# One ring of five PSUM places through the whole program

## The chip, the cores and the metric

The kernel runs on one core of a Trainium2 chip. The metric is the time of one execution on the device in microseconds; several executions are made and the median is given. Beside them one execution is recorded by the hardware profiler, with a start and a length for each instruction of each engine, and for each packet of each DMA queue.

The core has a matrix engine (TensorE, "PE" in the profile), a vector engine (VectorE, "DVE"), a scalar engine (ScalarE, "ACT"), GpSimd ("POOL") and a sync engine ("SP") that here only issues DMAs. TensorE writes its products to PSUM, which has eight banks; a tile of 128 x 512 float32 fills one bank. VectorE or ScalarE reads a product out of its bank, and only then may the next product be written there. Each engine works through its own instructions in a fixed order and waits on semaphores for the others.

## The reference

`x` is 4 x 1024 x 2048 in float32. The block is an adaptive-norm layer with two halves:

```python
mod = (silu(c) @ wmod).reshape(4, 6, 1, -1)            # c: 4 x 2048, wmod: 2048 x 12288
sa, ca, ga, sb, cb, gb = mod[:, 0] ... mod[:, 5]       # ga, gb held away from zero
h = layernorm(x) * (1 + ca) + sa
x = x + ga * (causal_conv(h, K) + D * h)               # K: 2048 taps of a state space model
h = layernorm(x) * (1 + cb) + sb
x = x + gb * (h @ W.T + bias + sum_e w_e (h @ A_e.T) @ Bf_e.T)
```

The convolution runs along the 2048 features of each of the 4096 tokens. `K` comes from 64 complex state parameters by a Cauchy sum at 2048 frequencies and an inverse Fourier transform. The feed forward half has one 2048 x 2048 matrix `W` and sixteen low-rank updates of rank 16.

## The kernel before

The work is done in two stages, and TensorE does nearly all of it as float16 pairs: a float32 operand is split into a high part and a low residue, and three products (high-high, high-low, low-high) stand for one.

*Modulation.* `section(sec)` (sections 0 to 5) does sixteen steps; a step loads a 1 MB tile `wm` of `wmod` from SP's queue and multiplies it in four column groups into `modps` (L325), one PSUM bank of its own. Six weight tiles are in stock for sections 1, 0 and 2, which come first; 4, 3 and 5 are spread over the later rows with three tiles. After the last step ScalarE copies `modps` to `mrow`, four transposes `mtp` (L339) turn it into columns, and VectorE makes `ca`. From `ca` the early scale `cae` is made (`early_scale`, by way of a maximum over partitions on GpSimd).

*The taps.* `toeplitz` runs `s4`, whose few products write `s4cs`, `s4sp`, `s4rp` and `s4kp`; the 2048 taps go to DRAM, `kd`, and come back in two halves as a matrix `kb` of shifted rows (GpSimd's queue, L261). Four products with a reversing matrix write `kbps` (L276); VectorE and ScalarE copy it back to `kb` and make the three float16 pairs `kh`, `kl` of the convolution's families.

*Convolution.* 32 rows of 128 tokens, r = 0 to 31. `conv_prep` normalises a row to `n`, transposes it in four groups of four 128 x 128 transposes, each group into a tile `tp` (L579); ScalarE reads the group in four instructions with the modulation's scale and shift into `t` (L583), VectorE adds pairs to `sm`, and both are split into `hc` and `hs`. `conv_mm` does two halves q of 1024 outputs; each half has three families of products (L616): family 0 into `ya`, which ScalarE copies to `qs` (L629); family 2 into `yb`, which VectorE adds to `qs`; then family 1 onto the same `ya`. So a tile `ya` lives through all three families. A family in the first half has 12 products, 1280 columns times three; in the second half it has 24. VectorE applies the gate and adds `x`. `conv_post` stores the row to DRAM, `x1d`, and sums its square on ScalarE (L666) for the second norm.

*Merging.* Between the rows `merges` prepares the low-rank factors and does eight chunks c: eight tiles `lps` of six low-rank products each (L494), which VectorE adds to the loaded weights `we` (L496); ScalarE scales them, and seven sums of quarter blocks go to DRAM as float16 pairs, `wcd`.

*Feed forward.* A unit u is 256 tokens; there are 16, done for two halves q of the columns. `left` transposes a unit's rows (tiles `tp`, L706) and makes the seven left operands; `ffn_unit` does the seven products of 24 matmuls each (L756) into three tiles X, Y and Z, with ScalarE and VectorE combining them. The first unit's `left` runs during rows 30 and 31 of the convolution.

*PSUM before.* In the first stage: two tiles for `ya` and two for `yb` (pool `cps`), three tiles in pool `tps` for everything else (`tp`, `mtp`, `lps`, `kbps` and the small products), one for `modps`. After the last row the pools are closed and two others opened: five tiles `acc` for the products of the feed forward, two `tps` for its transposes.

*What sets the order.* The program is written as generators that yield to each other (`PLAN` and `tick` say which part of the next row, of the merging or of the modulation is taken at which point of a row). A scheduler then orders each engine's instructions by priority and by its own estimate of when operands and tiles are ready, and it hands out the tiles of a pool to whatever it places next. `tc.issue_after` and `tc.high_priority` steer it in places; the taps' steps have high priority. So a change of pools changes the order in which instructions stand on each engine. What a tile's next user waits for is the last reader of the previous user.

Of the kernel before, what the change touches and what calls it, by code (L numbers as in the profile page):

```python
# [24 lines left out]
P = 128  # L25
# [9 lines left out]
class Net:  # L35
    def __init__(self, ctx, tc, io):
        self.ctx, self.tc, self.nc, self.io = ctx, tc, tc.nc, io
        self.cst = ctx.enter_context(tc.tile_pool(name="cst", bufs=1))
        self.dram = ctx.enter_context(tc.tile_pool(name="scr", bufs=1, space=DRAM))
    def psum(self, stack, name, bufs):  # L40
        return stack.enter_context(self.tc.tile_pool(name=name, bufs=bufs, space=PSUM))

    def const(self, name, shape, dt=F32):
        return self.cst.tile(shape, dt, tag=name, name=name)
# [30 lines left out]
    def s4(self, pool):  # L75
# [66 lines left out]

        nl = T([P, 2], "s4nl")
        tsc(nl, lam, -1.0, None, MUL)
        rp = self.tps.tile([P, 8, 16], F32, tag="t", name="s4rp")
        w = 512
        yield
        cps = [[self.cps.tile([P, w], F32, tag=t, name="s4cs") for t in ("pa", "pb")] for _ in range(2)]
        for n in range(2):
            for i, ps in enumerate(cps[n]):  # L150
                nc.tensor.matmul(ps, one, cs[:, i, ds(n * w, w)], start=True, stop=True)
# [83 lines left out]
    def toeplitz(self, pool):  # L235
        nc, v = self.nc, self.nc.vector
        rev = pool.tile([P, P], F32, tag="rev", name="rev")
        nc.gpsimd.memset(rev, 0.0)
        nc.gpsimd.affine_select(
            out=rev, in_=rev, compare_op=ALU.not_equal, fill=1.0, base=1 - P, pattern=[[1, P]], channel_multiplier=1  # L240
        )
        kk = pool.tile([P, 16], F32, tag="kk", name="kk")
        yield from self.s4(pool)
        v.tensor_copy(kk, self.kp)
        dt = pool.tile([1, 1], F32, tag="dt", name="dt")
        nc.scalar.dma_start(out=dt, in_=self.io["D"].unsqueeze(0))
        v.tensor_tensor(kk[0:1, 0:1], kk[0:1, 0:1], dt, ADD)
        m = pool.tile([P, 1], F32, tag="km", name="km")
        v.tensor_reduce(m, kk, AX.X, ALU.max, apply_absolute_value=True)
        s, self.kinv = self.pow2(self.cst, self.allmax(pool, m, 1, "km"), 1, "ks")  # L250
        v.tensor_scalar(kk, kk, s, None, MUL)
        kd = self.dram.tile([P + D], F32, tag="kd", name="kd")
        z = pool.tile([1, P], F32, tag="kz", name="kz")
        v.memset(z, 0.0)
        nc.gpsimd.dma_start(out=kd[0:P].unsqueeze(0), in_=z)
        nc.gpsimd.dma_start(out=kd[P:].rearrange("(a b) -> a b", b=16), in_=kk)

        kb = pool.tile([P, D], F32, tag="kb", name="kb")
        for h in range(2):
            src = bass.AP(tensor=kd.tensor, offset=kd.offset + 1 + 1024 * h, ap=[[1, P], [1, 1024]])  # L260
            nc.gpsimd.dma_start(out=kb[:, ds(1024 * h, 1024)], in_=src)  # L261
        self.kb = kb
        yield


        kv = kb.rearrange("p (m e t) -> p m e t", e=2, t=P)
        ev, od = kv[:, :, 0, :], kv[:, :, 1, :]
        kf, self.kf = {}, {}
        for f in (0, 2, 1):
            kf[f] = [self.kpool.tile([P, HC, P], F16, tag=f"k{x}{f}", name=f"k{x}{f}") for x in "hl"]  # L270
        for half in range(2):
            m = ds(4 * half, 4)
            for q in range(2):
                ps = self.tps.tile([P, 512], F32, tag="t", name="kbps")
                sl = ds(1024 * half + 512 * q, 512)
                nc.tensor.matmul(ps, rev, kb[:, sl], start=True, stop=True)  # L276
                (v.tensor_copy if q else nc.scalar.copy)(kb[:, sl], ps)
            for f in (0, 2, 1):
                hi, lo = (x[:, m] for x in kf[f])
                if f == 0:  # L280
                    src = ev[:, m]
                else:
                    src = pool.tile([P, 2, 512], F32, tag="kdif", name="kdif")
                    src = src[:, 0].rearrange("p (c t) -> p c t", t=P)
                    if f == 2:
                        v.tensor_tensor(src, od[:, m], ev[:, m], SUB)
                    elif half:
                        v.tensor_tensor(src, od[:, 3 : HC - 1], ev[:, m], SUB)
                    else:
                        v.tensor_scalar(src[:, 0:1], ev[:, 0:1], -1.0, None, MUL)  # L290
                        v.tensor_tensor(src[:, 1:], od[:, 0:3], ev[:, 1:4], SUB)
                nc.scalar.copy(hi, src)
                v.tensor_tensor(lo, src, hi, SUB)
            self.kf = {f: [x.rearrange("p m t -> p (m t)") for x in y] for f, y in kf.items()}
            yield
# [179 lines left out]
    def merge(self, pool, tmp, c):  # L475
        nc, v = self.nc, self.nc.vector
        lf = tmp.tile([P, 2, 2, P], F32, tag="laf", name="laf", bufs=2)
        nc.sync.dma_start(out=lf, in_=self.io["A"][c])
        la = tmp.tile([P, 2, 2, 2, P], F16, tag="lac", name="lac")
        for k in range(2):  # L480
            v.tensor_scalar(lf[:, k], lf[:, k], self.lsa[:, k : k + 1], None, MUL)
        nc.scalar.copy(la[:, 0], lf)
        v.tensor_tensor(la[:, 1], lf, la[:, 0], SUB)
        we = tmp.tile([P, 2, D], F32, tag="we", name="we")
        for h in range(2):
            nc.sync.dma_start(out=we[:, h], in_=self.io["WT"][ds(P * (c + HC * h), P), :])
        for h in range(2):
            for q in range(4):
                ps = self.tps.tile([P, 512], F32, tag="t", name="lps")
                osl = ds(512 * q, 512)  # L490
                n = 0
                for k in range(2):
                    for x, y in ((0, self.bh), (0, self.bl), (1, self.bh)):
                        nc.tensor.matmul(ps, la[:, x, k, h], y[:, k, osl], start=(n == 0), stop=(n == 5))  # L494
                        n += 1
                v.scalar_tensor_tensor(we[:, h, osl], ps, self.linv, we[:, h, osl], MUL, ADD)  # L496
                yield

        m = pool.tile([P, 4], F32, tag="wem", name="wem")
        for h in range(2):  # L500
            for q in range(2):
                j = tmp.tile([P, 1024], F32, tag="wct", name="wsq")
                i = 2 * h + q
                nc.scalar.activation(j, we[:, h, ds(1024 * q, 1024)], AF.Square, accum_out=m[:, i : i + 1])
        mm = pool.tile([P, 1], F32, tag="wmm", name="wmm")
        v.tensor_reduce(mm, m, AX.X, ADD)
        nc.scalar.activation(mm, mm, AF.Sqrt)
        s, inv = self.pow2(pool, mm, 1, "wes")
        for h in range(2):
            v.tensor_copy(self.winv[:, c + HC * h : c + HC * h + 1], inv)  # L510
            for q in range(2):
                sl = ds(1024 * q, 1024)
                nc.scalar.activation(we[:, h, sl], we[:, h, sl], AF.Copy, scale=s)
            yield
        b11, b12 = we[:, 0, 0:1024], we[:, 0, 1024:2048]
        b21, b22 = we[:, 1, 0:1024], we[:, 1, 1024:2048]

        def put(i, t):
            hl = tmp.tile([P, 2, 2, 512], F16, tag="wch", name="wch", bufs=2)
            tv = t.rearrange("p (q n) -> p q n", n=512)  # L520
# [12 lines left out]
        v.tensor_tensor(b12, b22, b12, SUB)  # L533
        put(6, b12)
        yield
        v.tensor_tensor(b11, b12, b11, ADD)
        put(5, b11)
        yield
        v.tensor_tensor(b21, b21, b11, SUB)
        put(3, b21)  # L540
        yield
# [55 lines left out]
    def conv_mm(self, pl, hs, x, tick, early, pace, y=None):  # L597
# [25 lines left out]

        for q in range(2):
            jj = slice(4 * q, 4 * q + 4)
            pa = self.cps.tile([P, 4, P], F32, tag="pa", name="ya")
            family(pa, 0, q, True)
            qs = pl["t"].tile([P, 4, P], F32, tag="qs", name="qs")
            self.lasta = nc.scalar.copy(qs, pa)  # L629
            tick()  # L630
            pb = self.cps.tile([P, 4, P], F32, tag="pb", name="yb")
            family(pb, 2, q, True)
            self.lastv = v.tensor_tensor(yv[:, jj, 1, :], pb, qs, ADD)
            if not early:
# [215 lines left out]
def net(ctx: ExitStack, tc: tile.TileContext, io):  # L850
# [8 lines left out]
    def pool(stack, name, bufs, side="left"):  # L859
        return stack.enter_context(tc.tile_pool(name=name, bufs=bufs, side=side, reuse_waits="tile"))  # L860

    left, right, p2, ps1 = ExitStack(), ExitStack(), ExitStack(), ExitStack()
    k.cps = k.psum(ps1, "cps", 2)
    k.tps = k.psum(ps1, "tps", 3)
    k.mps = k.psum(ps1, "mps", 1)
    pl = {}
    wmp = pool(right, "wm", WM, "right")
    msm = pool(right, "msm", 1, "right")
# [271 lines left out]
    gens = [next_left(1)]  # L1140
    take(gens[0], 1)
    left.close()
    ps1.close()
    k.acc = k.psum(p2l, "acc", ACC)
    k.tps = k.psum(p2l, "tps", TPS)

    for name in ("v", "o", "e", "g"):
        pr[name] = pool(p2l, "p2" + name, 5 if name == "o" else 1)
# [88 lines left out]
```

## Time and profile before

| | us |
|---|---|
| median of three executions | 2143.35 (2140.45 to 2143.99) |
| the profiled execution | 2143.08 |
| its span, first to last instruction | 2141.3 |
| convolution stage | 0 to about 920 |
| feed forward stage | about 920 to 2139 |

The engines' busy time is counted once where instructions overlap. Matmuls are pipelined, so the length shown for one (0.38 us for 512 columns) is longer than the distance to the next (0.213 us). A float32 product other than a transpose shows as two records, so a modulation step of four products shows as eight. A line of a timeline reads: start, length, engine, line, operation, what is written and read, shape, count, and in brackets the idle time before it with what ended it. A line of waits reads: who waited, for whom, us in total, times, the longest. A line by stretch gives, for PE, PEld (weight loads), DVE, ACT and POOL, the busy time and the count of instructions, and then the granted clock of TensorE, the mean busy share of the DMA engines, and GB/s.

### The profile page before, as it was taken

What the parts mean: (1) busy time and instruction counts of PE and PEld (TensorE: products, weight loads), DVE (VectorE), ACT (ScalarE), POOL (GpSimd) and SP (SyncE); (2) the same over time, 40 slices, a digit from 0 to 9 for tenths busy, and PEclk for the clock granted to TensorE, in tenths of its full rate; (3) what the DMA queues carried; (4) which work ended last, traced back from release to release, by engine and by line L of the source; (5) the groups of instructions that cost most, each with busy time, mean ns of one, the idle gap of its engine ahead of it and who ended that gap; (6) DMA issues with size and microseconds to landing.
All of it is one profiled execution on the core that took longest, in us unless ns stands there. A gap on an engine that the chain in (4) does not pass through costs nothing.

```text
span 2141.3 us, 28488 instructions
## 1 busy us (share of the span) xinstructions
PE 2075.5 (97%) x11121; PEld 1022.2 (48%) x11121; DVE 1310.7 (61%) x2360; ACT 924.9 (43%) x1703; POOL 7.2 (0%) x19
## 2 busy tenths in 40 slices
PE   6998999999999999999999999999999999999999
PEld 1434544554545555644545545545444444444444
DVE  6529889888998999756565565565432323332323
ACT  1425776765676768755454454555200000000000
POOL 0000000000000000000000000000000000000000
PEclk8999999999999999999999999999999999999999
DMA  9993768677775556387465564564794545555542
GB/s 402 421 382 136 262 236 298 218 280 284 298 255 197 186 203 246 133 335 274 180 242 188 190 240 180 202 239 178 270 353 162 188 154 171 164 164 167 177 154 73
DMA packets 127813, 486.22 MB, mean 227 GB/s; under 512 B 13672, under 2 KB 14088, under 8 KB 96446
## 3 DMA queue, kind: packets, MB, share of 16 engines
q1 hardware_dynamic: 126624, 479.65, 61.6%
q10 hardware_dynamic: 526, 2.63, 0.3%
q8 instruction: 87, 1.43, 0.3%
q0 software_dynamic: 528, 2.11, 0.2%
q14 instruction: 48, 0.39, 0.1%
HBM read 329.04 MB, written 155.30 MB: 226 GB/s over the span
## 4 chain that ended last, share of the span: by engine, by line
PE 61%; issue 27%; DVE 6%; DMA 3%; ACT 2%; SPq 0%; POOL 0%; POOLq 0%; DVEq 0%; ACTq 0%
PE fZ L756 23%; PE fX L756 15%; PE fY L756 15%; PE tp L706 3%; PE ya L616 2%; PE modps L325 2%; DMA wm<-in_wmod 1%; PE yb L616 1%; ACT t L583 1%; DMA x<-x1d 1%; DVE st L548 1%; DVE hc L594 0%; DVE lf L719 0%; DVE y L643 0%; ACT x L666 0%
## 5 line engine op out<-in xcount | busy, mean ns | idle before, releaser
L756 PEld LDWEIGHTS <-lf 128*128 128x128 f16 x5400 | 528.4, 98 | 621.2 <-issue 3.4
L756 PE MATMUL fZ<-w,lf 128*128 128x512 f16 (+1 forms) x2328 | 513.8, 377 | 1.3 <-ACT p L764 0.8
L756 PE MATMUL fX<-w,lf 128*128 128x512 f16 x1536 | 342.8, 379 | 1.4 <-DVE y L642 1.4
L756 PE MATMUL fY<-w,lf 128*128 128x512 f16 x1536 | 342.0, 379 | 0.0
L616 PEld LDWEIGHTS <-hc 128*128 128x128 f16 x2304 | 214.8, 98 | 212.4 <-issue 46.8
L774 DVE TENSOR_TENSOR xo<-xo,gb 128x512 f32<-128x512 f32 x128 | 87.6, 689 | 238.5 <-DMA xo<-x1d 226.4
L583 ACT ACTIVATE t<-tp,sa,ca 128x128 f32<-128x128 f32 x480 | 189.6, 476 | 38.8 <-PE tp L579 38.6
L616 PE MATMUL ya<-kh,hc 128*128 128x512 f16 (+3 forms) x768 | 192.2, 328 | 9.4 <-ACT qs L629 9.4
L616 PE MATMUL yb<-kh,hc 128*128 128x512 f16 (+3 forms) x768 | 193.4, 328 | 1.9 <-DVE hc L594 1.4
L616 PE MATMUL ya<-kh,hs 128*128 128x512 f16 (+3 forms) x768 | 194.6, 328 | 0.7 <-ACT y L640 0.7
L764 ACT COPY p<-fZ 128x512 f32<-128x512 f32 x64 | 37.2, 582 | 285.4 <-PE fZ L756 272.1
L616 PEld LDWEIGHTS <-hs 128*128 128x128 f16 x1152 | 107.2, 98 | 106.8 <-issue 28.3
L764 ACT COPY p<-fX 128x512 f32<-128x512 f32 x32 | 18.8, 586 | 317.9 <-PE fX L756 242.8
L708 ACT ACTIVATE gt<-tp,sb,cb 128x256 f32<-128x256 f32 x256 | 125.0, 576 | 62.4 <-PE tp L706 60.8
L325 PE MATMUL modps<-wm,sct 128*32 128x512 f32 x768 | 118.1, 653 | 17.1 <-DMA wm<-in_wmod 9.9
L616 PE MATMUL ya<-kl,hc 128*128 128x512 f16 (+3 forms) x384 | 125.7, 327 | 0.0
L616 PE MATMUL ya<-kl,hs 128*128 128x512 f16 (+3 forms) x384 | 125.6, 327 | 0.0
L616 PE MATMUL yb<-kl,hc 128*128 128x512 f16 (+3 forms) x384 | 125.6, 327 | 0.0
L779 DVE TENSOR_TENSOR fin<-fX,gb 128x512 f32<-128x512 f32 x32 | 22.1, 691 | 127.5 <-PE fX L756 127.4
L579 PE MATMUL tp<-ident,n 128*128 128x128 f32 x512 | 76.9, 276 | 16.2 <-DVE n L558 6.8
L594 DVE TENSOR_TENSOR hc<-t,hc 128x512 f16<-128x512 f32 x128 | 87.3, 682 | 7.2 <-ACT hc L593 7.0
L494 PE MATMUL lps<-lbh,lac 128*128 128x512 f16 x256 | 86.4, 380 | 4.8 <-DVE we L496 2.6
(274 smaller groups left out, 2219.8 us busy)
## 6 DMA issues: line engine op xcount, KB each, us to landing
wm<-in_wmod SPq DMA_DIRECT2D x96, 1024.0 KB, 8.3
lfd<-lf SPq DMA_DIRECT2D x112, 512.0 KB, 3.3
lf<-lfd SPq DMA_DIRECT2D x112, 512.0 KB, 3.9
x<-in_x SPq DMA_DIRECT2D x32, 1024.0 KB, 8.2
x1d<-y SPq DMA_DIRECT2D x32, 1024.0 KB, 5.2
x<-x1d SPq DMA_DIRECT2D x32, 1024.0 KB, 7.7
xo<-x1d SPq DMA_DIRECT2D x128, 256.0 KB, 3.7
out<-xo SPq DMA_DIRECT2D x127, 256.0 KB, 2.8
```

The source lines that it names most:

```text
L325: self.last = self.nc.tensor.matmul(self.modps[32 * g : 32 * g + 32, :], self.sct[:, j].rearrange("p r b -> p (r b)"), w[:, ds(512 * g, 512)],
L494: nc.tensor.matmul(ps, la[:, x, k, h], y[:, k, osl], start=(n == 0), stop=(n == 5))
L579: nc.tensor.transpose(tp[:, k], n[:, ds(P * (c0 + k), P)], self.ident)
L583: nc.scalar.activation(t[:, k], tp[:, k], AF.Identity, bias=self.sa[:, c, b : b + 1], scale=self.ca[:, c, b : b + 1],)
L594: self.lastlo = v.tensor_tensor(lo[:, sl], src, hi[:, sl], SUB)
L616: self.lastc = nc.tensor.matmul(pf[:, o:512], h, self.kf[f][z][:, ds(k0, 512 - o)], start=first, stop=(i == last and (x, z) == (1, 0)), sk ...
L706: nc.tensor.transpose(tp[:, c, r], xs[r][:, ds(P * (c0 + c), P)], self.ident)
L708: nc.scalar.activation(t[:, c0 + c], tp[:, c], AF.Identity, bias=self.sb[:, c0 + c, b : b + 1], scale=self.cb[:, c0 + c, b : b + 1],)
L756: nc.tensor.matmul(ps[name][:, cols], lf[i][:, k, x, :], wc[i][k // 4][:, k % 4, y, cols], start=(first and n == 0), stop=(n == 3 * HC - 1 ...
L764: nc.scalar.copy(t, ps[name])
L774: v.tensor_tensor(x, x, self.gbias[:, h], ADD)
L779: v.tensor_tensor(t, cv, self.gbt[:, h], MUL)
```

## The change

The pools of PSUM are opened once, for the whole program: a ring `acc` of five tiles, `tps` of two, `mps` of one. The families of the convolution (`ya`, `yb`), the low-rank products (`lps`), the reversing products (`kbps`) and the taps' `s4cs` and `s4rp` take tiles from `acc`, in one name "a" that the feed forward's X, Y and Z go on using. The transposes, and a few small products (`s4sp`, `s4kp`, `mtp`, `gsp`, `gst`, `gps`), stay in `tps`, which has two tiles instead of three in the first stage. The pools are no longer closed and opened between the stages. No instruction is added or removed.

```diff
+        self.acc = ctx.enter_context(tc.tile_pool(name="acc", bufs=ACC, space=PSUM))
+        self.tps = ctx.enter_context(tc.tile_pool(name="tps", bufs=TPS, space=PSUM))
+        self.mps = ctx.enter_context(tc.tile_pool(name="mps", bufs=1, space=PSUM))
...
-        rp = self.tps.tile([P, 8, 16], F32, tag="t", name="s4rp")
+        rp = self.acc.tile([P, 8, 16], F32, tag="a", name="s4rp")
...
-        cps = [[self.cps.tile([P, w], F32, tag=t, name="s4cs") for t in ("pa", "pb")] for _ in range(2)]
+        cps = [[self.acc.tile([P, w], F32, tag="a", name="s4cs") for _ in range(2)] for _ in range(2)]
...
-                ps = self.tps.tile([P, 512], F32, tag="t", name="kbps")
+                ps = self.acc.tile([P, 512], F32, tag="a", name="kbps")
...
-                ps = self.tps.tile([P, 512], F32, tag="t", name="lps")
+                ps = self.acc.tile([P, 512], F32, tag="a", name="lps")
...
-            pa = self.cps.tile([P, 4, P], F32, tag="pa", name="ya")
+            pa = self.acc.tile([P, 4, P], F32, tag="a", name="ya")
...
-            pb = self.cps.tile([P, 4, P], F32, tag="pb", name="yb")
+            pb = self.acc.tile([P, 4, P], F32, tag="a", name="yb")
...
-    k.cps = k.psum(ps1, "cps", 2)
-    k.tps = k.psum(ps1, "tps", 3)
-    k.mps = k.psum(ps1, "mps", 1)
...
-    ps1.close()
-    k.acc = k.psum(p2l, "acc", ACC)
-    k.tps = k.psum(p2l, "tps", TPS)
```

`ACC` is 5 and `TPS` is 2, as before.

More of the change, by code (lines that the diff above doesn't have):

```diff
@@ L39, in __init__ @@
         self.dram = ctx.enter_context(tc.tile_pool(name="scr", bufs=1, space=DRAM))
-    def psum(self, stack, name, bufs):
-        return stack.enter_context(self.tc.tile_pool(name=name, bufs=bufs, space=PSUM))
+        self.acc = ctx.enter_context(tc.tile_pool(name="acc", bufs=ACC, space=PSUM))
+        self.tps = ctx.enter_context(tc.tile_pool(name="tps", bufs=TPS, space=PSUM))
+        self.mps = ctx.enter_context(tc.tile_pool(name="mps", bufs=1, space=PSUM))
     def const(self, name, shape, dt=F32):
@@ L860, in pool @@
         return stack.enter_context(tc.tile_pool(name=name, bufs=bufs, side=side, reuse_waits="tile"))
-    left, right, p2, ps1 = ExitStack(), ExitStack(), ExitStack(), ExitStack()
-    k.cps = k.psum(ps1, "cps", 2)
-    k.tps = k.psum(ps1, "tps", 3)
-    k.mps = k.psum(ps1, "mps", 1)
+    left, right, p2 = ExitStack(), ExitStack(), ExitStack()
     pl = {}
```

## The prediction

> **What bounds the kernel now.** I read the page first, then TensorE's waits, then busy time by stretch, then TensorE's timeline at the start and around row 18.
>
> ```profile
> PE 2075.5 (97%) x11121; PEld 1022.2 (48%) x11121; DVE 1310.7 (61%) x2360; ACT 924.9 (43%) x1703; POOL 7.2 (0%) x19
> ```
>
> TensorE is busy for 97% of the span, and no product goes away: time moves only where TensorE's idle time grows or shrinks. Where that is, by stretch (PE busy, ..., granted clock, DMA share, GB/s):
>
> ```profile
> 0.00:50.00 50.00, 32.31 (x152) 5.97 (x152) 30.69 (x114) 6.98 (x11) 4.09 (x13) 0.86 0.98 400
> 50.00:150.00 100.00, 94.56 (x603) 39.86 (x603) 42.06 (x102) 33.94 (x92) 1.30 (x3) 0.97 0.99 403
> 150.00:300.00 150.00, 135.35 (x806) 72.32 (x803) 126.96 (x285) 97.58 (x208) 1.06 (x2) 0.95 0.59 219
> 300.00:920.00 620.00, 599.02 (x3686) 321.84 (x3685) 550.24 (x1131) 437.22 (x889) 0.78 (x1) 1.00 0.65 239
> 920.00:2141.00 1221.00, 1214.29 (x5884) 582.20 (x5881) 560.76 (x730) 349.22 (x505) 0.00 (x0) 1.00 0.57 201
> ```
>
> From 920 us on (feed forward) only 7 us are idle, and the change leaves that stage's places as they were. The stage before it idles for about 59 us, 18 of them before 50 us. What those waits are (us in total, times, longest):
>
> ```profile
> PE ya L616 <- ACT qs L629: 9.4, 8, 2.3
> ...
> PE tp L579 <- ACT t L583: 5.8, 3, 2.8
> PE tp L579 <- DVE we L496: 3.5, 3, 1.6
> ...
> PE lps L494 <- DVE we L496: 2.6, 2, 1.9
> PE lps L494 <- ACT t L583: 2.2, 4, 0.6
> ```
>
> All but the first line are waits for a PSUM place, since `tp` and `lps` share three tiles; so is the first feed forward product's wait for VectorE's `y` (1.4 us, once).
>
> **The change, part by part.** Four parts.
>
> (1) *Low-rank products leave the transposes' ring.* The place waits above sum to 5.8+3.5+2.6+2.2+1.4 = 15.5 us. I count them all as removed: in the new ring each `lps` takes a place whose last reader lies 7 to 13 us of TensorE work back. The changed order also puts six low-rank products (1.28 us) and four transposes (0.5 us) ahead of the second products of rows 10, 15 and 20, which waited for `qs` for 1.89, 0.83 and 0.82 us: 3.5 us. Removed: 19.0 us.
>
> (2) *Transposes have two tiles, not three.* Each group of four transposes now waits until ScalarE has read the group two before it, twice per row. Row 18 shows what that costs (timeline of TensorE, then of ScalarE: start, length):
>
> ```profile
> 552.93 0.61 PE L579 MATMUL tp<-ident,n 128*128 128x128 f32 x4
> ...
> 558.97 1.14 ACT L583 ACTIVATE t<-tp,sa,ca 128x128 f32<-128x128 f32 x3
> ```
>
> The first group ends at 553.5. ScalarE does a 2.00 us square and a 1.04 us cast in between; two of the three reads shown are this group's last, and they end at about 559.8: 6.2 us later. The changed order has about 3.95 us of work between the first and the third group (24 products of the families, four transposes, one matmul of wmod). The third group will stall for about 2.3 us. I did the same for every new wait: the reader's delay behind TensorE, as in the trace of before, less the work that the changed order puts between (0.213 us per 512 columns, 0.125 us per transpose, 1.0 us per wmod step), less stalls already counted in between. Rows 1 and 2: 1.4 us. Rows 4 to 8: 3.2+1.5+1.5+0.9+1.0 = 8.1. Rows 8 and 9, where ScalarE prepares the low-rank factors in pieces of 2 us: 3 us, my choice, between 0 and the 8.8 that the delay of before (17.9 us behind TensorE) would give. Rows 10 to 20: 14.4. Rows 23 to 30: 3.6. The first feed forward unit's transposes, done during row 30: 5.6. Sum 36 us. The same working on the order of before gives 27 us for the place and `qs` waits where the trace shows 19, because ScalarE catches up whenever TensorE stands. So I take 36 x 19/27 = 25 us. Ends: 12 (half of it) and 36.
>
> (3) *Reversing products early.* In the order of before the four reversing products (`kbps`) stand behind the first section's last wmod steps. The start of before (TensorE's timeline with [idle before], and GpSimd's line for the load):
>
> ```profile
> 36.32 1.94 PE L325 MATMUL modps<-wm,sct 128*32 128x512 f32 x8
> 40.88 1.93 PE L325 MATMUL modps<-wm,sct 128*32 128x512 f32 x8 [2.63 <-DMA wm<-in_wmod]
> ...
> 48.36 1.06 PE L325 MATMUL modps<-wm,sct 128*32 128x512 f32 x8 [0.92 <-DMA wm<-in_wmod]
> 50.13 0.66 PE L339 MATMUL mtp<-ident,mrow 128*128 128x128 f32 x4 [0.71 <-ACT mrow L336]
> 52.57 1.96 PE L276 MATMUL kbps<-kb,rev 128*128 128x512 f32 x4 [1.78 <-DMA kb<-kd]
> ...
> 44.51 1.07 POOL L261 DMA_DIRECT2D kb<-kd  x2 [4.89 <-DMA kd<-kk]
> ```
>
> With places of their own, the scheduler now puts the first `kbps` right behind the step at 36.32, ahead of the last four steps, and the other three between those four. TensorE works in order, and `kb` is issued at 44.51 and lands at 52.5. So TensorE stands from 38.3 to 52.5, and behind it stand four wmod steps, the column transpose `mtp`, and, through `ca` and the early scale, ScalarE's first scaling of transposes. Laid out: 52.5, four `kbps` at 0.95 = 3.8, four steps at 1.06 = 4.2, two of these at the 1.94 of a cold start instead: +1.8, copy `mrow` 0.65: `mtp` at 63.0 instead of 50.13. From there `cae` is ready after 5.3 us as before (55.4 less 50.1). Then ScalarE scales two groups (8 x 0.27), casts 0.6+0.45, and VectorE's residue and one wmod step follow: 5 us. The first convolution product starts at about 73.3 instead of 62.43: +11. It restarts cold after another 7 us without much work: +1. I take 12 us. Ends: 7 (`kb` lands by 48, since TensorE's standing also stops the reloading of weight tiles, whose loads fill the DMA engines at a 0.98 share) and 16 (cold restarts, and a late first cast). Nothing gives it back: from 57 us on TensorE does not wait for weights, the later chains (`gsp`, `gps`, `n` of row 4) follow TensorE, and the work behind is the same. Moved past on the other queues: the four copies of `kbps` go ahead of the early scale on VectorE and ScalarE (0.6 to 0.7 us each); SP's weight loads wait for tiles that come free up to 14 us later, with six tiles in stock. GpSimd's queue is unchanged.
>
> The granted clock was 0.51 from 33 to 47 us, and 1.00 from 47 on. [...]
>
> (4) *Convolution families in the ring of five; feed forward tiles from the same ring.* A family now waits for a VectorE eviction of some earlier tile instead of its own. By the working of (2) three of these stall, after rows 10, 15 and 20 (2.4, 1.0 and 0.7 us), and are in the 14.4. The first feed forward product no longer waits for a new pool (its 1.4 is in (1)). From 920 us on the order is the same: 0.
>
> [...]
>
> **Sum.** -19 + 25 + 12 = +18. The profiled execution took 2143.08 us (span 2141.3 and 1.8 around it), within 0.3 us of the median of 2143.35. Predicted: 2161 us, from 2152 to 2169 if this case holds.
>
> **Rivals.**
> - *Places balance out.* (2) comes at its low end, 12: -19+12+12 = +5, 2148. For it: ScalarE is busy for 70% of 300 to 920 us and gets time to catch up. Against: a row's backlog comes from squares and casts that return every row.
> - *ScalarE's backlog in full*: 36, and 16 at the start: -19+36+16 = +33; with parts of both 2172. For it: rows 4 to 9 have ScalarE at its busiest. Against: the same working overstated before.
> - *The stall at the start is hidden* because the weights (share 0.98 to 0.99 until 150 us) set the pace there: only -19+25 = +6 or less, 2143 to 2149. Against: TensorE waits for no weight after 50 us.
> - *Faster*: the two tiles suffice, because ScalarE reads them as TensorE does them, so that (2) is under 2 us: -19+2+12 = -5, 2138. It decides if ScalarE's delay behind a transpose falls under about 4 us in most rows; it was 6.2 in row 18.
> - *The change does nothing*: excluded, the order of the first 900 us differs.
>
> **How the numbers follow.** Likeliest case 0.56; places balance 0.17; backlog in full 0.12; hidden start 0.09; faster 0.06. The range 2147 to 2171 leaves out the faster case, most of the hidden start and half of the full backlog, some 0.19. No change that can be told apart is 0.2%, 4.3 us: faster is the faster case, 0.06; the same is most of the hidden start and a rest of the balance, 0.09; slower the rest, 0.85.
>
> **What would show it.** Part 3: TensorE idle for 10 us or more ahead of `kbps`, waiting for DMA `kb`, first `ya` near 73 us. Part 1: the lines `lps` <- `t` and `tp` <- `we` gone. Part 2: `tp` <- ACT `t` grown from 5.8 to 20 us or more. If the first `ya` starts before 66 us, or `tp` <- `t` stays under 10, I am wrong.

## The result and the profile after

The changed kernel takes 2147.01 us (median of 20 executions) against 2143.49 us for the kernel before on the same chip: a ratio of 1.0017, 95% interval 1.0010 to 1.0024, so it is slower by 2 to 5 us. Forecast were 2161 us and a range of 2147 to 2171, at whose lower edge the time lies. The sign was right, the size was not: +18 was worked out, +3.5 came, less than the 4.3 us below which the forecast called two times the same. The profiled execution took 2148.56 us (span 2146.8).

The page's line for TensorE, after:

```profile
PE 2071.3 (96%) x11121; PEld 1019.4 (47%) x11121; DVE 1311.5 (61%) x2360; ACT 927.0 (43%) x1703; POOL 7.7 (0%) x19
```

TensorE does the same 11121 products in a span that is 5.5 us longer. Busy time by stretch after (columns as before: PE, PEld, DVE, ACT, POOL, granted clock, DMA share, GB/s):

```profile
0.00:50.00 50.00, 24.68 (x120) 5.17 (x120) 30.69 (x114) 6.48 (x10) 4.10 (x13) 0.86 0.97 398
50.00:150.00 100.00, 86.57 (x550) 34.43 (x551) 39.02 (x95) 35.06 (x92) 1.66 (x3) 0.92 0.90 352
150.00:300.00 150.00, 137.18 (x827) 71.42 (x827) 118.50 (x272) 89.03 (x187) 1.16 (x2) 0.97 0.62 230
300.00:920.00 620.00, 602.17 (x3708) 322.63 (x3707) 557.08 (x1141) 443.38 (x908) 0.78 (x1) 0.99 0.65 240
```

Up to 150 us TensorE is busy for 111.3 us, where it was busy for 126.9 before: 15.6 us are lost there. From 150 to 920 us it is busy for 739.4 us against 734.4: 5 us are won. TensorE's timeline shows the loss (start, length; the idle time before it in brackets):

```profile
37.71 1.06 PE L326 MATMUL modps<-wm,sct 128*32 128x512 f32 x8
54.17 2.08 PE L277 MATMUL kbps<-kb,rev 128*128 128x512 f32 x2 [15.39 <-DMA kb<-kd]
56.18 3.59 PE L326 MATMUL modps<-wm,sct 128*32 128x512 f32 x16
59.70 2.84 PE L277 MATMUL kbps<-kb,rev 128*128 128x512 f32 x6
62.47 1.92 PE L326 MATMUL modps<-wm,sct 128*32 128x512 f32 x16
65.10 0.65 PE L340 MATMUL mtp<-ident,mrow 128*128 128x128 f32 x4 [0.71 <-ACT mrow L337]
...
76.36 0.51 PE L617 MATMUL ya<-kh,hs 128*128 128x512 f16 x1
```

`mtp`, at 50.13 before, starts at 65.10, and the first convolution product at 76.36 instead of 62.43. The waits of TensorE after (us in total, times, longest):

```profile
PE kbps L277 <- DMA kb<-kd: 15.4, 1, 15.4
...
PE tp L580 <- ACT t L584: 12.1, 11, 4.8
PE ya L617 <- ACT qs L630: 10.5, 7, 4.6
PE tp L580 <- DVE n L559: 4.8, 3, 3.0
PE tp L580 <- ACT t L589: 4.7, 2, 3.5
...
PE lps L495 <- DVE lac L484: 1.3, 1, 1.3
```

The waits of `lps` on `t` and of `tp` and `lps` on `we` are gone, as forecast. The wait of transposes on ScalarE's `t` has grown from 5.8 to 12.1 us, not to 20 or more. That is neither the 20 that was to confirm part 2 nor the under 10 that was to refute it. (The 4.7 us on L589, the scaling of the first rows, come with the late start: e2 below, which has three tiles, shows 3.5 of them.) The wait for `qs` is no smaller than the 9.4 of before.

When the same product starts in the two executions, after less before, is the quickest account of where time goes. Beside it stand some of the experiments that follow (us; the last column is the best kernel found). Each column is one execution, and executions of one kernel lie up to 15 us apart (e1's was 3.8 us above its median), so a few us between two columns are no sign of the kernels:

| product, and when it started before | after | e1 | e2 | e5 | e7 | e12 |
|---|---|---|---|---|---|---|
| first `ya`, 62.4 | +13.9 | +2.5 | +9.5 | +1.3 | +2.2 | +1.2 |
| row 3, 174.5 | +9.2 | +2.2 | +14.5 | +2.4 | +0.5 | +4.7 |
| row 9, 329.9 | +11.4 | +3.3 | +14.4 | +5.1 | +2.5 | -4.2 |
| row 16, 529.3 | +4.1 | -4.9 | +11.9 | +3.5 | -0.6 | -11.9 |
| row 22, 690.5 | +1.4 | -7.6 | +11.6 | +4.1 | -0.4 | -15.9 |
| first `fX`, 922.5 | +4.2 | -4.1 | +12.9 | +4.7 | +0.4 | -14.6 |

After loses 13.9 us at the start and wins 9.8 back by the first feed forward product. The forecast had +12 and then +6 more.

### The profile page after: what moved, and what is told of

The parts are those of the page before. It is cut to its first block, busy times and chain, and to the rows that moved or that the text cites. A ratio compares the mean times of both kernels' runs of the same rounds, so it can differ in the third digit from the quotient of the medians.

```text
span 2146.8 us, 28488 instructions
## 1 busy us (share of the span) xinstructions
PE 2071.3 (96%) x11121; PEld 1019.4 (47%) x11121; DVE 1311.5 (61%) x2360; ACT 927.0 (43%) x1703; POOL 7.7 (0%) x19
## 4 chain that ended last, share of the span: by engine, by line
PE 69%; DVE 15%; ACT 7%; DMA 6%; issue 2%; SPq 0%; POOL 0%; DVEq 0%; ACTq 0%; POOLq 0%
PE fZ L757 22%; PE fY L757 15%; PE fX L757 15%; PE ya L617 6%; PE yb L617 3%; PE modps L326 3%; PE tp L707 2%; ACT t L584 2%; DVE st L549 2%; PE lps L495 2%; ACT x L667 1%; DVE wch L523 1%; DVE y L644 1%; DVE hc L595 1%; DMA x<-in_x 1%
## 5 line engine op out<-in xcount | busy, mean ns | idle before, releaser
L617 PE MATMUL ya<-kh,hc 128*128 128x512 f16 (+3 forms) x768 | 193.4, 330 | 10.5 <-ACT qs L630 10.5
L765 ACT COPY p<-fX 128x512 f32<-128x512 f32 x32 | 18.7, 586 | 316.8 <-PE fX L757 241.7
L580 PE MATMUL tp<-ident,n 128*128 128x128 f32 x512 | 79.6, 281 | 22.0 <-ACT t L584 12.1
L780 DVE TENSOR_TENSOR fin<-fX,gb 128x512 f32<-128x512 f32 x32 | 22.1, 692 | 127.8 <-PE fX L757 127.7
L549 DVE BATCH_NORM_STATS2 st<-x 128x6 f32<-128x512 f32 x128 | 84.2, 681 | 7.1 <-DMA x<-in_x 7.1
```

Of the source, the lines that this page charges most:

```text
L549: v.bn_stats(st[:, q], x[:, ds(512 * q, 512)])
L580: nc.tensor.transpose(tp[:, k], n[:, ds(P * (c0 + k), P)], self.ident)
L617: self.lastc = nc.tensor.matmul(pf[:, o:512], h, self.kf[f][z][:, ds(k0, 512 - o)], start=first, stop=(i == last and (x, z) == (1, 0)), sk ...
L765: nc.scalar.copy(t, ps[name])
```

## The experiments

Every kernel was timed beside the kernel before, whose median was 2142.1 to 2142.8 us (2143.5 beside after). "Against before" below is the ratio less 1, times 2143.

| run | ring / transposing tiles | `lps` in | `kbps` | median | ratio (95%) | against before |
|---|---|---|---|---|---|---|
| before | 2+2 / 3 | tiles | late | 2143.5 | | |
| after | 5 / 2 | ring | early | 2147.0 | 1.0017 (1.0010 to 1.0024) | +3.6 |
| e1 | 5 / 2 | ring | late | 2136.4 | 0.9973 (0.9961 to 0.9985) | -5.8 |
| e2 | 2+2 / 3 | tiles | early | 2156.4 | 1.0066 (1.0050 to 1.0082) | +14.1 |
| e3 | 4 / 3 | ring | early | 2161.8 | 1.0086 (1.0070 to 1.0103) | +18.4 |
| e4 | 4 / 3 | ring | late | 2149.3 | 1.0031 (1.0018 to 1.0044) | +6.6 |
| e5 | 2+2 / 2 | tiles | late | 2146.9 | 1.0016 (1.0006 to 1.0027) | +3.4 |
| e6 | 2+2 / 3 | families' places | late | 2148.2 | 1.0030 (1.0017 to 1.0043) | +6.4 |
| e7 | 5 / 2 | tiles | late | 2141.7 | 0.9994 (0.9982 to 1.0005) | -1.3 |
| e8 | 4 / 2 | ring | late | 2148.1 | 1.0026 (1.0013 to 1.0038) | +5.6 |
| e9 | 5 / 2, order only | ring | late | 2138.7 | 0.9980 (0.9970 to 0.9989) | -4.3 |
| e10 | 6 / 1 | ring | late | 2169.2 | 1.0123 (1.0110 to 1.0136) | +26.4 |
| e11 | 7 for all | ring | late | 2134.2 | 0.9960 (0.9948 to 0.9972) | -8.6 |
| e12 | 7 for all, then 5 / 2 | ring | late | 2127.8 | 0.9927 (0.9910 to 0.9945) | -15.6 |

### The start: e1, e2, e9

e1 is the kernel after with `kbps` in the transposes' tiles again; the scheduler then puts it behind `mtp`, as in before.

```diff
-                ps = self.acc.tile([P, 512], F32, tag="a", name="kbps")
+                ps = self.tps.tile([P, 512], F32, tag="t", name="kbps")
```

> The kernel after, with the four reversing products (kbps) taken from the transposes' tiles again, as before; ring of five and two transposing tiles stay. That puts kbps behind the first section's last modulation products again (behind mtp). Theory A (delays add up: the stall at 54 us is carried to the end, and the rest of the change is worth what the shift curve shows between the first ya and the first fX, -9.8 us): the 15.4 us wait on DMA kb goes, first ya back near 62 to 64 us instead of 76.3, and the whole time is 2147.0 - 13.9 = 2133 (2130 to 2137). Theory B (the later start lets ScalarE and VectorE get ahead, and that is what gave the 9.8 us back; without the stall the row stalls come back): first ya near 62 to 64 too, but the shift grows again over rows 0 to 25, TensorE waits on ACT t and DVE n grow from 17 and 5 us by about 8 to 10, and the time is 2141 to 2146.

e2 is the kernel before with only `kbps` moved; `kbps` then stands early, as in after.

```diff
-                ps = self.tps.tile([P, 512], F32, tag="t", name="kbps")
+                ps = self.cps.tile([P, 512], F32, tag=("pa", "pb")[q], name="kbps")
```

> The kernel before, with kbps alone moved to the convolution's four places (cps, tags pa and pb); low-rank products stay with the transposes' three tiles. kbps then stands ahead of 16 of the first section's modulation products, as in the kernel after. Theory A (the stall is carried to the end): TensorE waits some 15 us for DMA kb, first ya at 76 us, time 2143.5 + 13.9 = 2157 (2153 to 2160). Theory B (the rows give it back whatever the places are): first ya at 76 us, but the waits lps<-ACT t, tp<-ACT t and tp<-DVE n of the rows shrink by 8 to 10 us, and the time is 2145 to 2149.

e9 is the kernel after with one rule of order and no place changed.

```diff
+    mtp = k.last
     p = prep(0, False)
...
-        with tc.issue_after(k.mrow.ins), tc.issue_after(k.lastn.ins):
+        with tc.issue_after(k.mrow.ins), tc.issue_after(k.lastn.ins), tc.issue_after(mtp.ins):
```

> The kernel after whole (ring of five with kbps in it, two transposing tiles), with one line of order: the reversing products are issued behind the first section's last transposes (mtp). No place is changed. If the order alone, not the place, makes the start late: wait on DMA kb under 2 us, first ya within 2 us of before, time as e1_rev_back, 2134 to 2138; kbps no longer takes transposing tiles, so a few us less are possible. If the place in the ring itself costs (kbps holding ring places that ya wants): above 2139.

Measured: 2136.4, 2156.4 and 2138.7 us. Theory A holds in e1 and e2. Two lines of TensorE's waits in e1, then one of e2:

```profile
PE tp L580 <- ACT t L584: 10.2, 11, 4.8
...
PE kbps L277 <- DMA kb<-kd: 1.3, 1, 1.3
```

```profile
PE kbps L276 <- DMA kb<-kd: 15.5, 1, 15.5
```

In e2 the first `ya` came at 71.9, not at 76, but by row 3 the delay was 14.5 us, and it is carried through the whole convolution: +12.9 at the first `fX`, +14.1 in the end. So the rows do not give a late start back, and the 9.8 us that after won after its first product came from the rest of the change. e1 shows the same from the other side: first `ya` 11.4 us earlier than in after, and 8.2 us left of it at the first `fX` (e9: 11.4 and 12.1). The row waits on `t` stayed at 10.2 (12.1 in after), so theory B, in which the late start itself had shortened them, falls. e9 lies a little above the 2134 to 2138 expected, its wait on `kb` was 2.6 us, not under 2, and its first `ya` was 2.5 us behind that of before; its interval overlaps that of e1. With every place as in after and only the order changed, the wait goes from 15.4 to 2.6 us: the order makes the start late, not the place.

### Four places and three tiles: e3, e4

```diff
-ACC, TPS = 5, 2
+ACC, TPS = 4, 3
```

e3 has `kbps` early as after, e4 late as e1.

> The kernel after with four places in the ring and three transposing tiles through the whole program (so in the feed forward section too, which had five and two in both kernels); kbps early as in the kernel after. Theory A (the two tiles cost what the rows' waits on ACT t show, 12.1 + 1.0 us against 5.8 before, and shortage of ring places costs nothing): 5 to 8 us less in rows 0 to 30 than after, 2139 to 2142, if the feed forward section, with four ring places in place of five, loses nothing; each us lost there shows behind 920 us as waits of fX on its readers. The prediction's step of +25 us for the two tiles would give 2122 if it were right. Theory B (the tiles are not what the rows wait for): 2145 to 2149.

> As the run before (four places, three transposing tiles), and kbps taken from the transposes' tiles again, so that the start has the order of before. Against the kernel before this leaves the low-rank products in the ring, any free place for ya and yb, and the feed forward section with four places and three tiles. Theory A (delays add): the low-rank step's -19 us come out whole if the prediction's step was right, 2125; with the step sized by what the kernel after gave back between first ya and first fX plus what three tiles save (-9.8 - 5 to 8), 2126 to 2129. Theory B (rows give back only what the start lost): 2141 to 2146.

Measured: 2161.8 and 2149.3 us, above every theory. Giving the transposes their third tile back at the price of the fifth ring place costs some 13 us on top of e1 (2136.4 to 2149.3). TensorE's waits in e4:

```profile
PE ya L617 <- ACT qs L630: 22.1, 11, 7.3
...
PE yb L617 <- DVE we L497: 4.1, 3, 1.6
PE tp L580 <- ACT t L584: 2.8, 2, 2.0
```

The third tile does what was asked of it: transposes wait 2.8 us for `t` instead of 10.2. But `ya` waits 22.1 us for `qs` where it waited 10.5 in e1, and `yb` waits for `we`, the reader of a low-rank product that had its place. Together the two lines grow by 15.7 us, where the transposes save 7.4. The ring's size, which the forecast put at 0, is a term.

### One term at a time: e5, e6, e7, e8

e5 is the kernel before with two transposing tiles, one bank left unused:

```diff
-    k.tps = k.psum(ps1, "tps", 3)
+    k.tps = k.psum(ps1, "tps", 2)
```

> The kernel before with two transposing tiles instead of three in the convolution part, the bank left over unused; low-rank and reversing products stay in those two tiles, the convolution's four places stay as they are, the start keeps its order. This prices the second step of the prediction alone. The prediction's step (ScalarE's delays of before stay what they are): +25 us, and the low-rank products find two tiles in place of three, so 2168 or more. Theory C (the two tiles cost what TensorE's waits on ACT t showed in the kernel after, about 7 us, and the low-rank products wait longer for the same two tiles, 1 to 2 us more for each place wait of before): 2152 to 2162. Theory D (a third tile is worth nothing, since TensorE is held elsewhere): 2142 to 2146.

e6 is the kernel before with `lps` in the families' four places:

```diff
-                ps = self.tps.tile([P, 512], F32, tag="t", name="lps")
+                ps = self.cps.tile([P, 512], F32, tag=("pa", "pb")[q % 2], name="lps")
```

> The kernel before with the low-rank products (lps) alone moved, from the transposes' three tiles to the convolution's four places (tags pa and pb, by turns); everything else as before. This prices the first step of the prediction alone, on four places. The prediction's step: place waits of lps, tp and fX and three row waits go, 2143.5 - 19 = 2124.5. Theory C (four places shared by ya, yb and lps are too few: ya waits for qs and yb for the readers of lps, as the run with four places and three tiles through the whole program showed with 22.1 and 4.1 us and 2149): 2146 to 2152, waits of ya on ACT qs over 18 us.

e7 is e1 with `lps` in the two transposing tiles as well:

```diff
-                ps = self.acc.tile([P, 512], F32, tag="a", name="lps")
+                ps = self.tps.tile([P, 512], F32, tag="t", name="lps")
```

> The kernel after with the reversing and the low-rank products both in the transposes' two tiles, so that the ring of five serves ya and yb (and the feed forward products) alone. Against e1_rev_back (2136.4) only the low-rank products move back. The prediction's first step (19 us for the low-rank products leaving the tiles, more with two tiles): 2155 to 2165, waits lps<-ACT t, lps<-DVE we, tp<-DVE we back with 15 us or more. Theory D (the move of lps is worth little, the fifth place is what helps): 2136 to 2142 with ya<-ACT qs under 5 us.

e8 is e1 with `ACC, TPS = 4, 2`.

> The kernel of e1_rev_back with four ring places instead of five, two transposing tiles, one bank unused through the whole program (the feed forward part too). Against e1_rev_back it prices the fifth place, against e4_ring4_tp3_rev_back (2149.3) the third transposing tile. Theory C (each has its own price: the fifth place 13 us plus the tile's 7, so that 13 is what is left after them): fifth place about +20, third tile about 7: 2155 to 2158, waits ya<-ACT qs near 22 us and tp<-ACT t near 10. Theory D (the third tile is worth nothing, all of the 13 us is the fifth place): 2148 to 2151. The prediction (tile 25, ring place 0) would have 2136 here.

Measured: 2146.9, 2148.2, 2141.7 and 2148.1 us. e5 is nearest to theory D, 3.4 us above before (1.3 to 5.8): two tiles in place of three cost a seventh of the 25 us forecast, although the low-rank products shared them. TensorE's waits in e5:

```profile
PE tp L579 <- ACT t L583: 11.5, 9, 4.8
...
PE ya L616 <- ACT qs L629: 6.1, 6, 2.1
...
PE tp L579 <- DVE we L496: 3.6, 4, 1.2
```

The wait on `t` doubles, as in after, while `qs` falls from 9.4 to 6.1 and the waits of `lps` from 4.8 to 0.4. e6 came as theory C said, with 17.1 us where over 18 were expected: on two pairs of places the low-rank products lose 6 us by leaving the tiles, and `ya` waits 17.1 us for `qs`. e7 and e8 came nearest to theory D, e7 at the upper end of its range and with 5.3 us of `qs`, not under 5. With `lps` still in the tiles, going from two pairs to one ring of five wins 4.7 us (e5 to e7); moving `lps` into that ring wins 4.5 more (e7 to e1). With `lps` in the ring, the fifth place is worth 11 us (e8 to e1), and of the 8.0 us that e8 is behind e1 at the first `fX`, 6.8 stand in four lines: `qs` 1.6, `yb` on `we` 3.5 and on `y` 1.2, `ya` on `y` 0.5. With four ring places the third transposing tile is worth nothing that the runs can tell (e8 +5.6, e4 +6.6). The waits that low-rank products cause in e7 by standing in the transposes' tiles:

```profile
PE tp L580 <- DVE we L497: 3.3, 5, 1.2
...
PE lps L495 <- DVE we L497: 0.9, 3, 0.5
```

Idle time alone does not carry these differences. The page's line for TensorE in e5:

```profile
PE 2083.0 (97%) x11121; PEld 1020.9 (48%) x11121; DVE 1311.3 (61%) x2360; ACT 925.7 (43%) x1703; POOL 7.0 (0%) x19
```

In its span of 2145.5 us TensorE idles for 62.5 us, 3.3 less than before, and is busy for 7.5 us more with the same products; the half-clock stretches account for only 0.7 of these. One place where they go shows in the timelines: up to the first `fX` and at full clock, the family products directly ahead of a group of transposes last 6.0 us longer in sum than their columns need (0.213 us per 512), against 2.4 us before, 11.0 in e10 and 0.5 in e12. The reading that fits is that a wait that is over before the shown end of the product ahead shows as busy time (512 columns are shown as 0.38 us, and the next product can start after 0.213), so that the lines of waits come out too short.

### More places, fewer tiles: e10, e11, e12

e10 is e1 with `ACC, TPS = 6, 1`. e11 puts every product but `modps` into one ring of seven (each `self.tps.tile(..., tag="t", ...)` becomes `self.acc.tile(..., tag="a", ...)`, `ACC = 7`); `kbps` then stands behind `mtp` without help.

> The kernel of e1_rev_back with six ring places and a single transposing tile. The runs so far price the fifth place at 5 us (low-rank products outside the ring) to 12 us (inside), and the third transposing tile at 1 to 4 us at most. If places in the ring go on paying and transposes hide: 2128 to 2134. The prediction's way of costing (every ScalarE delay of before frozen, one tile in place of two) would put over 40 us on top: 2176 and more; with one tile each group of transposes waits for the eviction of the one before it, some 64 groups in rows 1 to 31 at about 1 us of eviction (0.8 us more where two rows' groups meet), so a middle value is 2150 to 2190. Taken here: 2150 to 2190, waits tp<-ACT t over 25 us.

> All seven banks one ring: transposes, modulation columns, reversing, low-rank, convolution and feed forward products take the next of seven places. kbps stands behind mtp in this order. Theory C (what the runs priced is how long a writer waits for the reader of the place it gets, and seven places put that reader seven tiles back): waits tp<-ACT t and ya<-ACT qs both fall, 2128 to 2136. Theory E (a ring in strict turn makes short tiles wait behind long ones: a transposing group's place is held by a ya or yb that is read late): waits of tp on qs, y or we appear, over 15 us together, and the time is 2140 to 2155.

e12 is e11 up to the last row, and then the two pools of five and two that the kernel before has. As a change to the kernel before (`self.tt` is the tile's name, and every tile of the first stage but `modps` comes from `self.tps`):

```diff
-    k.cps = k.psum(ps1, "cps", 2)
-    k.tps = k.psum(ps1, "tps", 3)
+    k.tps, k.tt = k.psum(ps1, "ring", 7), "a"
...
-    k.tps = k.psum(p2l, "tps", TPS)
+    k.tps, k.tt = k.psum(p2l, "tps", TPS), "t"
```

> The kernel of e11_ring7 through the convolution part (all seven banks one ring), and five ring places and two transposing tiles in pools of their own for the feed forward part, as the kernel before has them there. In e11_ring7 the first feed forward product (fX) came 17.0 us earlier than in before, and the span ended only 8.9 us earlier. If the feed forward part lost the other 8 us by having its transposes in the common ring: 2143 - 17 = 2126 (2123 to 2129, some 1 to 2 us of waits at the change of pools in it). If the 17 us were only work put off behind the first fX, it comes back whatever the feed forward part's places are: 2132 to 2136.

Measured: 2169.2, 2134.2 and 2127.8 us. e10's time lies within what was expected, for another reason. At its first `fX` it is 9.8 us ahead of before, 4.5 of them convolution products that were only put behind that `fX`: with a sixth place beside it, a single transposing tile costs the convolution nothing that shows. All of the loss, some 34 us by the spans, comes behind the first `fX`. TensorE's waits in e10:

```profile
PE tp L580 <- ACT t L584: 7.8, 21, 1.3
PE tp L707 <- ACT gt L709: 6.4, 12, 1.3
PE fZ L757 <- ACT p L765: 4.2, 2, 3.4
...
PE ya L617 <- ACT qs L630: 1.3, 2, 0.7
```

The transposes of the convolution wait 7.8 us in 21 short waits, not over 25, and the wait for `qs` all but goes. In the feed forward part the transposes (L707) and `fZ` wait; these lines show 10.6 of the 34 us. From the first `fX` to the end, e10 and then before:

```profile
912.66:2165.70 1253.04, 1234.31 (x5908) 582.33 (x5905) 568.01 (x735) 361.11 (x509) 0.00 (x0) 1.00 0.56 197
```

```profile
922.50:2141.30 1218.80, 1213.20 (x5872) 581.28 (x5871) 558.29 (x727) 348.26 (x504) 0.00 (x0) 1.00 0.57 201
```

TensorE idles for 18.7 us there against 5.6, which is 13 of the 34 us; the other 21 stand as busy time, the 4.5 that were put off and, for some 10 us, products directly ahead of transposes: the groups of eight are split in two, and the product ahead of one takes 0.30 us (121 times) where it took 0.22 (63 times). e11's time is that of theory C, but not its waits: `qs` did not fall (11.8 us, against 10.5 in e1 and 9.4 before), and why seven places win is not shown by the lines of waits. e11 was 17.0 us ahead of before at the first `fX` and only 8.9 at the end; its feed forward part waited like this:

```profile
PE tp L706 <- ACT x L696: 3.8, 2, 2.4
PE fX L756 <- ACT p L764: 2.3, 1, 2.3
```

e12 keeps 14.6 us at the first `fX` and 14.0 at the end of its span; neither line is among TensorE's waits there, which come to 1.3 us behind 915 us. It is 15.6 us faster than before (11.8 to 19.3), and 19 faster than after. So the loss of e11 in the feed forward part was due to the common ring there. Of the 14.0 us by which its span is shorter than that of before, idle time gives 7.8 and busy time 6.2 (2069.3 against 2075.5).

## Why the prediction came out as it did

Going from before to after by way of e5, e7 and e1, each step changes one term, and the steps add up to the whole (against before, by the ratios, each uncertain by about 3 us; another way round could price the terms otherwise):

| step of the prediction | forecast | measured |
|---|---|---|
| (2) two transposing tiles, before to e5 | +25 (12 to 36) | +3.4 |
| (4) ring of five for the families, e5 to e7 | 0 | -4.7 |
| (1) `lps` leaves the tiles, e7 to e1 | -19 | -4.5 |
| (3) `kbps` early, e1 to after | +12 (7 to 16) | +9.4 |
| sum | +18 | +3.6 |

*Step (2) failed*, and it failed in its size: it alone is 22 us too high, and the measured 3.4 lies below its own low end of 12. The mechanism is there. Transposes do wait more on ScalarE, 12.1 us against 5.8. But the working took "the reader's delay behind TensorE, as in the trace of before" for a given, and the delay is not one. Measured over all 128 groups of four transposes, from the end of a group's last transpose to the end of ScalarE's last read of it, it is on average (us):

| groups that end at | three tiles (before) | two (e5) | two (after) | one (e10) |
|---|---|---|---|---|
| 0 to 150 us | 3.15 | 2.41 | 2.93 | 1.50 |
| 150 to 300 us | 5.91 | 4.91 | 4.99 | 3.37 |
| 300 to 640 us | 4.25 | 3.77 | 3.89 | 2.65 |
| 640 to 925 us | 5.06 | 4.47 | 4.59 | 2.87 |

With fewer tiles the delay is shorter in every stretch.

What that does to the step can be worked out from the traces. For each group, take the delay that it had before, less the time that lay in e5 between this group and the one two later, the stall itself left out; where that is positive it is a forecast stall. The sum is 21.6 us (27.8 in the order of after), near the 25 of the step. With e5's own delays in place of before's it is 11.3 us, and the wait line shows 11.5. For the single tile of e10 the two sums are 188 and 6.7 us, and the line shows 7.8. So the delay taken from before is what failed. The rest of the way from 11.5 to 3.4: before had 5.8 us of this wait already, and other waits shrank, by 3.3 us for `qs` and 4.4 of `lps`, while `yb` on `hc` grew by 2.9 and the busy time as told under e5.

The reading that fits the shorter delays: a group is written later, nearer to the time at which ScalarE comes to it, and part of the delay of before was only that the third tile let TensorE run ahead. Row 18, the example of the prediction, after (TensorE's first and third group, then ScalarE's work; the first two reads and two of the three last are those of the first group):

```profile
558.38 0.60 PE L580 MATMUL tp<-ident,n 128*128 128x128 f32 x4
...
564.02 0.66 PE L580 MATMUL tp<-ident,n 128*128 128x128 f32 x4 [0.35 <-ACT t L584]
```

```profile
559.07 0.46 ACT L584 ACTIVATE t<-tp,sa,ca 128x128 f32<-128x128 f32 x1
...
560.36 0.47 ACT L584 ACTIVATE t<-tp,sa,ca 128x128 f32<-128x128 f32 x1
561.18 2.00 ACT L667 ACTIVATE x<-y,mn 128x2048 f32<-128x2048 f32 x1 [0.35 <-DVE mn L665]
563.09 0.18 ACT L667 ACTIVATION_READ_ACCUMULATOR x<-y,mn 128x1 f32 x1
563.18 1.14 ACT L584 ACTIVATE t<-tp,sa,ca 128x128 f32<-128x128 f32 x3
```

The same square is in the way, but ScalarE's last read of the first group ends at about 564.0, 5.0 us behind it instead of 6.2. The third group has 4.7 us of work between (558.99 to 563.67) instead of the 3.95 worked out, and stalls for 0.35 us where 2.3 were forecast. The correction by 19/27, for ScalarE catching up, went in the right direction and by far not far enough. The premise at the head of the forecast, that time moves only where TensorE's idle time grows or shrinks, did not hold either: e5 has less idle time than before and takes longer.

*Step (1) was oversized too*, by 14.5 us. Its sum of place waits counted 5.8 us of `tp` on `t` as removed, of which half or more stays when the transposes have three tiles without `lps` (2.8 us in e4, 3.5 in e3, 4.1 in e6), and 3.5 of `qs`, which came back elsewhere (10.5 us in after). Of what low-rank products cause by sharing the tiles, e7 shows 4.2 us (`tp` on `we` 3.3, `lps` on `we` 0.9), near the 4.5 that moving them was worth. That a wait line is long did not make it a price.

*Step (4)* was called free and is a gain of 4.7. The places also decide what step (1) is worth: on two pairs of places, with three tiles, the same move costs 6.4 (e6), on a ring of five, with two, it wins 4.5. Why five suffice where four do not is argued, not shown: with a place free, the scheduler can put low-rank products between a row's family 2 and its family 1, which must wait for the copy `qs`.

*Step (3)* was right in mechanism, place and size. The stall was 15.39 us, `kb` came at 54.17 instead of 52.5, since the taps were 1.6 us later in this execution (its load was issued at 46.08, not 44.51), `mtp` stood at 65.10 against 63.0, and the first `ya` at 76.36 against 73.3. The +1 for a cold restart was the author's estimate, with no run ahead of the forecast that shows it; in after the four transposes at 73.45 took 1.11 us and the wmod step at 74.50 took 1.94, where those just before took 0.66 and 1.07, and the granted clock was 0.50 from 73.2 to 76.6 us. The price is 8 to 14 us by four pairs: 14.1 added to before, 9.4 and 7.9 taken off after, 11.8 between e3 and e4. "Nothing gives it back" held within a few us. The errors of (1) and (2), 14.5 and 21.6 us, have opposite signs and partly cancel; that is luck, and without it the time would have been further off.

Of the rivals, "places balance out" named the right time (2148) by the same luck, with the two tiles at 12 instead of 3 and the low-rank products at -19 instead of -9 for (1) and (4) together. The faster rival was nearest on the two tiles (under 2 us, against 3.4), and named its condition: a delay under about 4 us in most rows. That was met narrowly: by the mean of a row's four groups in 18 of 32 rows of after (15 before), and in 81 of the 128 groups (57 before). It missed the time (2138) because (1) and (4) together were worth 9.2 us and not 19. A late start hidden by the weights is refuted by e2.

## What to carry to other kernels

A reader's delay in a trace is not a fixed cost: here it shrank with every tile taken away (from 640 to 925 us 5.06 us with three tiles, 4.47 with two in e5, 2.87 with one), so price places by running the program with one fewer or one more, not by adding up frozen delays or place waits. When tiles move to another pool, look first at where the scheduler now puts their writers in each in-order engine's stream: four products placed ahead of their data cost 8 to 14 us here, nearly what the best division of the banks won, and one rule of order took it back. Sizes that suit one stage may not suit the next: seven places in common were best for the convolution and wrong for the feed forward part, and giving that part five and two of its own was worth 5 to 7 us (by spans and by ratios).

## What the runs showed of the chip beyond that

The clock of TensorE stayed low for longer after the stall than the working had it. Busy time and granted clock by stretch, after (granted clock is the third figure from the end):

```profile
39.00:54.00 15.00, 0.00 (x0) 0.00 (x0) 5.51 (x15) 0.20 (x1) 1.82 (x3) 0.50 1.02 423
54.00:59.60 5.60, 5.43 (x18) 1.10 (x18) 0.00 (x0) 0.00 (x0) 0.00 (x0) 0.50 0.54 201
59.60:66.00 6.40, 5.69 (x34) 2.33 (x30) 1.82 (x3) 1.54 (x4) 0.00 (x0) 1.00 0.97 358
```

From 54.17 TensorE worked without a break, and the clock was still 0.50 until about 59.6: 5.4 us of work at half speed. Two `kbps` products took 2.08 us and two wmod steps 3.59, where the same took 1.10 (before, at 56.36) and 1.92 (after, at 62.47) at full clock: 2.7 us lost, where the prediction had 1.8. The clock record has this stretch at half from 39.1 to 59.6 us, 20.5 us in all. It is the longest: the other half-clock stretches inside before and after last 3.4, 6.8, 10.2 and 13.7 us. What brings the clock back is not shown by these runs.

The same order of products also ran at either clock. In before four `kbps` took 1.96 us after a wait of 1.78, at a granted clock of 1.00. In e9 (0.50 from 53 to 58 us) they took 3.78 us after a wait of 2.55, and in e1, whose clock was at half from 38.6 us on, 3.75 after a wait of only 1.31. TensorE's lines, first of before, then of e9, then of e1:

```profile
52.57 1.96 PE L276 MATMUL kbps<-kb,rev 128*128 128x512 f32 x4 [1.78 <-DMA kb<-kd]
```

```profile
53.46 3.78 PE L277 MATMUL kbps<-kb,rev 128*128 128x512 f32 x4 [2.55 <-DMA kb<-kd]
```

```profile
53.31 3.75 PE L277 MATMUL kbps<-kb,rev 128*128 128x512 f32 x4 [1.31 <-DMA kb<-kd]
```

The four took 1.8 us longer there, and the first `ya` of e1 and e9 came 2.5 us later than that of before; in e12, whose `kbps` took 3.78 us too, it came 1.2 us later. So a difference of 1 to 2 us between two single traces at the start is no sign of the change.
